# Where the inner products of a two-level Strassen stand, and when the next matrix's quarters are loaded, in a graph layer with gated update

## The chip, the cores and the metric

One core of one Trainium2 chip. The metric is the device time of one execution in microseconds (us); the median of several runs is compared. All arithmetic on the layer's values is in 32-bit floats.

## The reference

A relational graph layer with a gate, on 1250 nodes of 1024 features, 20000 edges of 8 types:

```
h = relu(layernorm(x))
u = h @ root + bias
for r in range(8):
    mask = (edge_type == r)
    sums = segment_sum(h[src] * mask, dst);  cnt = segment_sum(mask, dst)
    u = u + (sums / max(cnt, 1)) @ weight[r]
z = concat(u, h) @ w_gate + b_gate
out = x + tanh(u) * z + h * (1 - z)
```

The kernel multiplies first and gathers after: `y[r] = h @ weight[r]` for all nodes, and each node then adds the rows of y that its edges name, each with its weight.

## The kernel before

**Eleven matrix products.** h (1250 rows, ten blocks of 128) is multiplied by eleven matrices of 1024x1024: the eight of `weight` (s = 0 to 7), `root` (s = 8), the lower half of `w_gate` (s = 9), and at the end the gathered u by its upper half. For each s, `step(s, i)` (line 361) runs over five pairs i = 0 to 4 of two row blocks; a pair is a 2x2 block matrix against the 2x2 quarters of the weight, and `product` (line 262) computes it with seven products (Strassen in Winograd's form) instead of eight. A product is 4 matmuls of 128x512, and each of these, in 32-bit floats, shows as two records in the profile. The seven, by the part of h that they read, and the names that the changed code gives them: A11 first, S1 fifth, S2 sixth, S4 third, S3 seventh, A12 second, A22 fourth. They go into two PSUM banks, b (A11, S2, S3, A22, one on top of the other) and c (S1, S4). ACT copies b after A11 (line 290), S2 (298), S3 (308) and A22 (334), and c after S1 (294); DVE adds c after S4 (303) and the copy of S3 (309). A bank that is added to again must first have been copied. Six banks go round.

**The inner level.** For s > 0 the product A12 of pairs 0 and 1, and that of pairs 2 and 3, are taken together: two row blocks against a quarter of the weight, b21, which `Second` (line 176) splits again into 2x2 and computes with seven inner products of 2 matmuls of 128x256 each (line 210). Its right sums t1 to t4 (128x512, line 194) and left sums s1 to s4 (128x256, line 200) are made by DVE, and its results are added by DVE to the rows of both pairs (line 214). All seven inner products stand in the odd pair (1 or 3), between its outer products; the generator `products` hands them out. The even pair runs A11, S1, S2, S3, S4, A22 with nothing between; the odd pair the same with the inner ones between. Pair 4 and all of s = 0 run all seven outer products in the order A11, S1, S2, S4, S3, A12, A22.

**Weights.** `Factors` (line 123) keeps nine buffers of 1 MB. A matrix needs seven: quarters b11, b12 (in the place of t3), b21, b22 and the sums t1 to t4 (lines 160 to 174, 128x2048 on DVE). The other two are the scratch of `Second`: f0 for its right sums, f1 for its left sums and copies of results. They become b11 and t3 of the next matrix. b11, b22 and b21 are loaded over ACT's queue, b12 over SP's.

**What sets the order.** The program is written out in the order in which each engine runs it. After each outer product (and after two of the inner groups of an odd pair) `done` calls `between(j)`, with j counted from 0 in each pair; `beside` in `step` uses these calls to place everything else:

- call 0 of pair 0: t4 (line 174), then, in pairs 0 and 2, the right sums (pair 0) and the left sums of `Second`
- call 6 of pair 3: both loads b11 and b12 of the next matrix; calls 0 and 3 of pair 4: b22 and b21; calls 3, 4 and 5: t1, t2, t3
- call 6 of an odd pair: the store of the even pair's first row block; the other row blocks are stored when their pair ends
- and at each call the other work's next piece (`on` or `spread`): in s = 0 to 3 the index work (ranks of edges in their nodes: bf16 counts on PE, lines 726 and 777, with work of DVE and ACT around them, lines 708 to 801), and from s = 4 on the gathers of y (POOL's indirect DMA, line 979, and DVE's weighted addition, line 987, through four buffers)

A pair has 7 calls, with s > 0 an even one 6 and an odd one 8 (`calls`, line 355).

Of the kernel before, what the change touches and what calls it, by code (L numbers as in the profile page):

```python
# [19 lines left out]
def tile_rgcn_highway(  # L20
# [31 lines left out]
    nc = tc.nc  # L52
# [9 lines left out]
    Q = D // 2  # L62
    H = Q // 2
    ND = -(-N // P)
    NP = ND // 2
# [3 lines left out]
    R0 = (0, 3, 6, R)  # L69
# [47 lines left out]
    def bank():  # L117
        return psum.tile([P, 512], F32, name="ps", bufs=6)
# [4 lines left out]
    class Factors:  # L123
# [12 lines left out]
        def load_first(self):  # L136
            old = self.old
            if old is None:
                free = wbuf
                self.place = dict(b11=free[0], t3=free[1], b22=free[2], t1=free[3], t2=free[4],  # L140
                                  b21=free[5], t4=free[6])
                self.spare = free[7:]
            else:
                p = old.place
                self.place = dict(b11=old.spare[0], t3=old.spare[1], b22=p["b11"], t1=p["t1"],
                                  t2=p["t2"], b21=p["b22"], t4=p["t3"])
                self.spare = [p["b21"], p["t4"]]
            p = self.place
            self.of = {A11: p["b11"], A12: p["b21"], S4: p["b22"], S1: p["t1"], S2: p["t2"],
                       S3: p["t3"], A22: p["t4"]}  # L150
            self.load(0, 0, p["b11"])
            self.load(0, 1, p["t3"], nc.sync)

        def load_b22(self):
            self.load(1, 1, self.place["b22"])
# [20 lines left out]
    class Second:  # L176
# [14 lines left out]
            self.a11, self.a12, self.a21, self.a22 = [  # L191
                h_op[i + o][:, A12, k:k + 2] for o in (0, 1) for k in (0, 2)]

        def right(self):
            nc.vector.tensor_sub(self.t1, self.b12, self.b11)
            nc.vector.tensor_sub(self.t2, self.b22, self.t1)
            nc.vector.tensor_sub(self.t3, self.b22, self.b12)
            nc.vector.tensor_sub(self.t4, self.b21, self.t2)

        def left(self):  # L200
            nc.vector.tensor_add(self.s1, self.a21, self.a22)
# [4 lines left out]
        def products(self, to):  # L206

            def add(p, a, b, fresh=False):
                for k in range(2):
                    nc.tensor.matmul(p, a[:, k, :], b[:, k, :], start=(fresh and k == 0),  # L210
                                     stop=(k == 1), skip_group_check=True)

            def more(of, a):
                nc.vector.tensor_add(of, of, a)  # L214

            b, c, a = [bank()[:, :H] for _ in range(3)]
            lo, hi = slice(0, H), slice(H, Q)
            add(b, self.a11, self.b11, True)
            nc.scalar.copy(self.p1_p6[:, lo], b)
            add(c, self.s1, self.t1, True)  # L220
            nc.scalar.copy(self.p5, c)
            yield
            add(b, self.s2, self.t2)
            nc.scalar.copy(self.p1_p6[:, hi], b)
            add(c, self.s4, self.b22)
            yield
            add(b, self.s3, self.t3)
            nc.scalar.copy(self.p7, b)
            add(a, self.a12, self.b21, True)
            more(to[0][:, :Q], self.p1_p6)  # L230
            more(to[0][:, hi], c)
            yield
            add(b, self.a22, self.t4)
            more(to[0][:, lo], a)
            more(to[1][:, hi], self.p5)
            more(to[1][:, hi], self.p7)
            yield
            more(to[1][:, lo], b)
            yield

    def transposed(aop, part, of, n):

# [17 lines left out]
            nc.vector.tensor_sub(aop[:, S3], aop[:, A11], aop[:, A21])  # L260

    def product(aop, w, to, between=lambda j: None, last=None, pieces=1, whole=True,
                second=None):

        c11, c12 = to[0][:, :Q], to[0][:, Q:]
        c21, c22 = to[1][:, :Q], to[1][:, Q:]
        step = [0]  # L270

        def add(b, i, fresh=False, at=slice(0, Q)):
            for k in range(KQ):
                nc.tensor.matmul(b[:, at], aop[:, i, k, :], w.of[i][:, k, at],  # L274
                                 start=(fresh and k == 0), stop=(k == KQ - 1),
                                 skip_group_check=True)

        def done():
            between(step[0])
            step[0] += 1  # L280

        def beside(call=False):
            if second is not None:
                next(second)
                if call:
                    done()

        b, c = bank(), bank()
        add(b, A11, True)
        nc.scalar.copy(c11, b)  # L290
        done()
        beside()
        add(c, S1, True)
        nc.scalar.copy(c22, c)  # L294
        done()
        beside(True)
        add(b, S2)
        nc.scalar.copy(c12, b)  # L298
        done()
        beside(True)  # L300
        def p3():
            add(c, S4)
            nc.vector.tensor_add(c12, c12, c)  # L303

        def p7():
# [10 lines left out]
        beside()  # L316
        done()
        if whole:
            d = p7()
        else:  # L320
            p3()
        beside()
        done()
        if whole:
# [17 lines left out]
        done()  # L342

    mats = [weight[r] for r in range(R)] + [root, w_gate[D:, :], w_gate[:D, :]]
    ROOT = R
    NM = len(mats)
    fac = []
# [3 lines left out]
    def paired(s, i):  # L351

        return s > 0 and i < NP // 2 * 2

    def calls(s, i):

        return 7 if not paired(s, i) else 8 if i % 2 else 6

    waiting = {}

    def step(s, i, between=lambda j: None):

        t = [rows.tile([P, D], F32, name="row") for _ in range(2)]
        two = paired(s, i)
        odd = two and i % 2 == 1
        if two and not odd:
            waiting["second"] = Second(fac[s], i)
            waiting["to"] = t[0]

        def put(i, part, t):  # L370
            d = i + part * NP
# [35 lines left out]
        second = waiting["second"].products((waiting["to"], t[0])) if odd else None  # L407
        product(h_op[i], fac[s], t, between=beside, whole=not two, second=second)
        for part in range(2):
            if part or not two or odd:  # L410
                put(i, part, t[part])

    steps = iter([(s, i) for s in range(NM - 1) for i in range(NP)])
# [77 lines left out]
    with ExitStack() as early:  # L491
# [85 lines left out]
        nc.scalar.activation(warm, eps, AF.Sqrt)  # L577
        x0 = [load_x(0, part, pieces=2 - part) for part in range(2)]
        fac[0].load_first()
        fac[0].load_b22()  # L580
        x1 = [load_x(1, 0, scratch(NP - 2, 0))]
        fac[0].load_b21()
# [371 lines left out]
    with ExitStack() as edges_part:  # L954
# [117 lines left out]
        def beside(e, total, s, i, last):  # L1072


            between = spread(e, total, sum(calls(a, b) for a in range(s, last + 1)
                                           for b in range(i if a == s else 0, NP)))
# [113 lines left out]
        def in_turn(*es):  # L1190
            for e in es:
                yield from e
# [62 lines left out]
        def held():  # L1255
# [7 lines left out]
            for add in old + new:  # L1263
                add()

        late = edges(LG, range(HELD, ND), to_last)
        between = spread(in_turn(late, held()), sum(K[LG]) + 2,
                         sum(calls(a, b) for a in range(s, NM - 1)
                             for b in range(i if a == s else 0, NP)))
        while s < NM - 1:  # L1270
            def beside_h(j):
                between(j)
# [69 lines left out]
```

## Time and profile before

| what | value |
|---|---|
| median of 3 runs | 1407.56 us (1400.13 to 1410.84) |
| profiled execution | 1407.21 us, its span 1405.4 us |
| mean granted clock of PE | 0.993 |
| PE busy, matmul records | 1361.3 us, 3786 |
| DVE / ACT / POOL busy | 930.0 / 365.2 / 634.6 us |
| line 274, outer products 128x512 | 2800 records with 16 of 128x256, 1237.9 us |
| line 210, inner products 128x256 | 504 records in two groups, 71.5 + 55.8 us |
| DMA | 272.78 MB, mean 194 GB/s |
| one weight quarter over ACT's queue | 1 MB, median 10.7 us from issue to landing |

The page gives each engine's busy time, the groups of instructions by line with the idle time before them and what ended it, and the DMA issues. A row of the timeline reads: start, length, engine, line, operation, output<-inputs, shape, count, and in brackets the idle time before it with the instruction that ended it. PE's matmuls overlap and their ends are modelled; from start to start is the safer measure. The matrices start about 120 us apart: s = 1 near 150, s = 4 near 537, s = 8 near 1020.

### The profile page before, as it was taken

How to read it: one execution, taken by the hardware profiler on the slowest of the kernel's cores; microseconds unless marked ns; L12 is line 12 of the kernel's file. 1: busy time of each engine (PE TensorE's matmuls, PEld its weight loads, DVE VectorE, ACT ScalarE, POOL GpSimd, SP SyncE). 2: the span in 40 equal slices, each digit the busy share in tenths (PEclk: the TensorE clock that was granted, in tenths of full speed). 3: DMA queues.
4: the chain of work that ended last, by engine and by line, in shares of the span. 5: the costliest groups of instructions: out<-in, count | busy, mean ns of one | idle time of the engine just before them, and what ended most of it. 6: DMA issues, size and time to landing. Idle time of an engine off the chain costs nothing.

```text
span 1405.4 us, 12717 instructions
## 1 busy us (share of the span) xinstructions
PE 1361.3 (97%) x3786; PEld 659.0 (47%) x3786; DVE 930.0 (66%) x1842; ACT 365.2 (26%) x793; POOL 634.6 (45%) x567
## 2 busy tenths in 40 slices
PE   7999799999999999999999999999989999999997
PEld 3444354445544444454444445454434545454443
DVE  6946776897768817555555775655367475657985
ACT  3335465656631111111111111111111111121220
POOL 0003555566561543655674364544327333424641
PEclk9999999999999999999999999999999999999999
DMA  8764344846463375369679547777849753676761
GB/s 299 278 199 112 96 106 119 226 94 142 83 193 102 62 206 138 84 207 270 194 245 326 203 167 243 290 260 270 301 123 344 246 189 111 211 249 215 271 234 57
DMA packets 110011, 272.78 MB, mean 194 GB/s; under 512 B 25906, under 2 KB 27936, under 8 KB 109808
## 3 DMA queue, kind: packets, MB, share of 16 engines
q0 software_dynamic: 48864, 128.60, 28.6%
q1 hardware_dynamic: 45232, 111.86, 26.3%
q10 hardware_dynamic: 15840, 31.46, 7.3%
q8 instruction: 30, 0.49, 0.1%
q14 instruction: 45, 0.37, 0.1%
HBM read 214.20 MB, written 80.65 MB: 210 GB/s over the span
## 4 chain that ended last, share of the span: by engine, by line
PE 45%; issue 21%; DMA 10%; DVE 10%; POOL 8%; ACT 1%; POOLq 0%; DVEq 0%; ACTq 0%
PE ps L274 39%; DMA got<-y,idx 7%; PE ps L210 5%; POOL got L979 4%; DMA u<-u_dram,node 2%; DVE u L987 2%; POOL got L436 1%; POOL u_dram L442 1%; DMA got<-hr_dram,node 1%; DVE w L170 0%; DMA node_dram<-ids,pos_i 0%; PE ps_n L726 0%; DVE row L303 0%; DVE w L166 0%; DVE row L214 0%
## 5 line engine op out<-in xcount | busy, mean ns | idle before, releaser
L274 PE MATMUL ps<-w,h_op 128*128 128x512 f32 x2800 | 1237.9, 597 | 19.1 <-ACT row L298 15.2
L274 PEld LDWEIGHTS ps<-w,h_op 128*128 128x128 f32 x2800 | 527.4, 191 | 633.9 <-issue 593.3
L987 DVE SCALAR_TENSOR_TENSOR u<-got,w_of,u 128x1024 f32<-128x1024 f32 (+1 forms) x192 | 245.9, 1282 | 200.2 <-DMA got<-y,idx 198.0
L979 POOL DMA_INDIRECT got<-y,idx x202 | 253.5, 1255 | 242.7 <-DVE u L987 146.0
L805 POOL DMA_INDIRECT table<-row_col,at_i x157 | 176.0, 1121 | 163.2 <-DVE at_i L801 83.3
L334 ACT COPY row<-ps 128x512 f32<-128x512 f32 x50 | 29.3, 585 | 264.9 <-PE ps L274 259.2
L309 DVE TENSOR_TENSOR row<-row,part 128x512 f32<-128x512 f32 x55 | 37.9, 690 | 78.9 <-ACT part L308 78.6
L308 ACT COPY part<-ps 128x512 f32<-128x512 f32 x55 | 32.2, 585 | 196.5 <-PE ps L274 196.3
L303 DVE TENSOR_TENSOR row<-row,ps 128x512 f32<-128x512 f32 x55 | 37.6, 684 | 66.9 <-PE ps L274 46.5
L290 ACT COPY row<-ps 128x512 f32<-128x512 f32 x55 | 32.1, 585 | 165.6 <-PE ps L274 153.6
L210 PE MATMUL ps<-w,w 128*128 128x256 f32 x288 | 71.5, 381 | 0.0
L294 ACT COPY row<-ps 128x512 f32<-128x512 f32 x55 | 32.2, 585 | 146.9 <-PE ps L274 137.0
L298 ACT COPY row<-ps 128x512 f32<-128x512 f32 x55 | 32.2, 585 | 146.5 <-PE ps L274 146.5
L442 POOL DMA_INDIRECT u_dram<-u,node x20 | 29.6, 1480 | 77.9 <-DVE u L987 65.4
L210 PEld LDWEIGHTS ps<-w,w 128*128 128x128 f32 x288 | 54.1, 190 | 19.0 <-issue 13.4
L791 DVE SCALAR_TENSOR_TENSOR junk<-k_bc,key_col,before 128x128 f32<-128x128 int32 x157 | 54.9, 350 | 4.2
L210 PE MATMUL ps<-w,h_op 128*128 128x256 f32 x216 | 55.8, 381 | 1.2 <-DVE row L303 1.2
L731 DVE TENSOR_TENSOR seen<-seen,ps_n 128x110 f32<-128x110 f32 x157 | 42.2, 269 | 19.7 <-PE ps_n L726 15.4
L473 POOL DMA_INDIRECT node_dram<-ids,pos_i x30 | 37.8, 1261 | 38.4 <-issue 36.8
L708 ACT ACTIVATE is_lo<-io,less_lo 128x128 bf16<-128x128 f32 x157 | 50.1, 391 | 0.9 <-DVE row L309 0.9
L210 PEld LDWEIGHTS ps<-w,h_op 128*128 128x128 f32 x216 | 40.6, 190 | 20.6 <-issue 14.3
L859 DVE SCALAR_TENSOR_TENSOR junk<-v_bc,val,one 128x1280 bf16<-128x1280 f32 x30 | 46.5, 1550 | 2.4 <-DMA v_bc<-val_dram 1.7
(180 smaller groups left out, 946.7 us busy)
## 6 DMA issues: line engine op xcount, KB each, us to landing
y<-row SPq DMA_DIRECT2D x72, 512.0 KB, 7.6
w<-in_L_gnn_weight_dram ACTq DMA_DIRECT2D x21, 1024.0 KB, 10.7
w<-in_L_gnn_weight_dram SPq DMA_DIRECT2D x11, 1024.0 KB
k_bc<-keys_dram SPq DMA_DIRECT2D x39, 256.0 KB, 4.4
l_bc<-los_dram SPq DMA_DIRECT2D x39, 256.0 KB, 5.7
w<-in_L_gnn_w_gate_dram ACTq DMA_DIRECT2D x6, 1024.0 KB
h_dram<-h_op SPq DMA_DIRECT2D x9, 512.0 KB, 6.6
hr_dram<-row SPq DMA_DIRECT2D x9, 512.0 KB, 4.5
```

The source lines that it names most:

```text
L210: nc.tensor.matmul(p, a[:, k, :], b[:, k, :], start=(fresh and k == 0), stop=(k == 1), skip_group_check=True)
L274: nc.tensor.matmul(b[:, at], aop[:, i, k, :], w.of[i][:, k, at], start=(fresh and k == 0), stop=(k == KQ - 1), skip_group_check=True)
L309: nc.vector.tensor_add(c22, c22, d)
L442: ins = nc.gpsimd.indirect_dma_start(out=of, out_offset=bass.IndirectOffsetOnAxis(ap=at, axis=0), in_=frm, in_offset=None)
L473: ins = nc.gpsimd.indirect_dma_start(out=node_dram[g][:, :], out_offset=bass.IndirectOffsetOnAxis(ap=pos_i[:, g, d:d + 1], axis=0), in_=id ...
L708: nc.scalar.activation(is_lo[:, i, :], io, AF.Abs, bias=less_lo[:, c0 + i:c0 + i + 1])
L731: nc.vector.tensor_add(seen[j][:, i, :], was, p[:, i, :])
L791: nc.vector.scalar_tensor_tensor(junk, o["k_bc"][:, i, :], key_col[:, c:c + 1], before, op0=OP.is_equal, op1=OP.mult, accum_out=rank[:, c: ...
L805: ins = nc.gpsimd.indirect_dma_start(out=table[:, :], out_offset=bass.IndirectOffsetOnAxis(ap=at_i[:n, i:i + 1], axis=0), in_=row_col[:n, ...
L859: nc.vector.scalar_tensor_tensor(junk, v_bc[:, g, :], val[:, c:c + 1], one.to_broadcast([P, KEYS]), op0=OP.is_gt, op1=OP.mult, accum_out=p ...
L979: nc.gpsimd.indirect_dma_start(out=t[:n], out_offset=None, in_=y[g][:, :], in_offset=bass.IndirectOffsetOnAxis(ap=at[:n, d, k:k + 1], axis=0),
L987: nc.vector.scalar_tensor_tensor(u[:n], t[:n], w, u[:n], op0=OP.mult, op1=OP.add)
```

## The change

- In pair 0 the inner `second` (a12 by b21) moves from pair 1 to stand between S2 and S3. Pair 1 has the others at new places: first and fifth after A11, sixth and third after S1, seventh after S2, fourth after S3.
- Pairs 2 and 3 are divided: in pair 2, first and fifth stand between S2 and S3, sixth and third after S3, seventh after S4, fourth after A22; in pair 3, `second` stands between S2 and S3, and DVE's additions of the others to pair 3's rows come after A11.
- Each pair has 7 calls now; pair 0's extra one is after the inner second's place, pair 1's after sixth and third, pair 2's at its end, pair 3's after the inner second.
- The left sums for pair 2 move from call 0 of pair 2 to call 6 of pair 1. In s = 1 to 3 the right sums stand one at each of calls 0 to 3 of pair 0 and the left sums at call 4; from s = 4 on all stay at call 0.
- b11 of the next matrix is loaded at call 0 of pair 3 and b12 at call 2 (both at call 6 before); t1, t2, t3 are made at calls 1, 3, 4 of pair 4 (3, 4, 5 before). b22 and b21 stay at calls 0 and 3.
- The store of an even pair's first row block stands after S4 in pair 1 as before, and after S3 in pair 3.

```diff
-            self.load(0, 1, p["t3"], nc.sync)
+
+        def load_next(self):
+            self.load(0, 1, self.place["t3"], nc.sync)
...
-        def right(self):
-            nc.vector.tensor_sub(self.t1, self.b12, self.b11)
-            nc.vector.tensor_sub(self.t2, self.b22, self.t1)
-            nc.vector.tensor_sub(self.t3, self.b22, self.b12)
-            nc.vector.tensor_sub(self.t4, self.b21, self.t2)
+        def right(self, k):
+            to, a, b = ((self.t1, self.b12, self.b11), (self.t2, self.b22, self.t1),
+                        (self.t3, self.b22, self.b12), (self.t4, self.b21, self.t2))[k]
+            nc.vector.tensor_sub(to, a, b)
...
+        def sixth(self):
+            self.add(self.b, self.s2, self.t2)
+            nc.scalar.copy(self.p1_p6[:, H:], self.b)
+            self.add(self.c, self.s4, self.b22)
+
+        def seventh(self):
+            self.add(self.b, self.s3, self.t3)
+            nc.scalar.copy(self.p7, self.b)
+
+        def fourth(self):
+            self.add(self.b, self.a22, self.t4)
+
+        def second(self):
+            self.a = bank()[:, :H]
+            self.add(self.a, self.a12, self.b21, True)
...
+        def filled(name):
+            if fill and name in fill and fill[name]():
+                done()
...
         add(b, S2)
         nc.scalar.copy(c12, b)
         done()
-        beside(True)
...
+        filled("sixth")
         if whole:
             p3()
-        else:
-            p7()
...
+        else:
+            d = p7()
+            p3()
...
         def beside(j):
...
-            if two and not odd and j == 0:
-                if i == 0:
-                    waiting["second"].right()
-                waiting["second"].left()
-            if odd and j == 6:
-                put(i - 1, 0, waiting["to"])
-            if (s, i, j) == (0, 0, 3) or (s > 0 and i == NP - 2 and j == 6):
+            if two and i == 0:
+                sums(j)
+            if two and (i, j) == (1, 6):
+                Second(fac[s], 2).left()
+            if (s, i, j) == (0, 0, 3) or (s > 0 and (i, j) == (3, 0)):
                 new.load_first()
+            if (s, i, j) == (0, 0, 3) or (s > 0 and (i, j) == (3, 2)):
+                new.load_next()
             if i == NP - 1:
                 if j == 0:
                     new.load_b22()
+                elif j == 1:
+                    new.make_t1()
                 elif j == 3:
                     new.load_b21()
-                    new.make_t1()
+                    new.make_t2()
                 elif j == 4:
-                    new.make_t2()
-                elif j == 5:
                     new.make_t3()
             between(j)
...
+        def sums(j):
+            e = waiting[0][0]
+            for k in range(4) if s > R0[1] and j == 0 else (j,) if s <= R0[1] and j < 4 else ():
+                e.right(k)
+            if j == (0 if s > R0[1] else 4):
+                e.left()
+
+        fill = {}
+        if two:
+            e, to = waiting[i - i % 2]
+            if i == 0:
+                fill = dict(sixth=lambda: (e.second(), e.second_to_first(to)))
+            elif i == 1:
+                fill = dict(first=lambda: e.first(),
+                            fifth=lambda: (e.sixth(), True),
+                            sixth=lambda: (e.seventh(), e.to_first(to), 0)[-1],
+                            seventh=lambda: (e.fourth(), e.to_second(t[0]), 0)[-1],
+                            third=lambda: (e.fourth_to_second(t[0]), put(i - 1, 0, to), 0)[-1])
+            elif i == 2:
+                fill = dict(sixth=lambda: e.first(),
+                            seventh=lambda: e.sixth(),
+                            third=lambda: (e.seventh(), e.to_first(to), 0)[-1],
+                            fourth=lambda: (e.fourth(), True))
+            else:
+                fill = dict(first=lambda: (e.to_second(t[0]), e.fourth_to_second(t[0]), 0)[-1],
+                            sixth=lambda: (e.second(), True),
+                            seventh=lambda: (e.second_to_first(to), put(i - 1, 0, to), 0)[-1])
```

`to_first`, `to_second`, `second_to_first` and `fourth_to_second` are DVE's additions of the inner results to the rows, the same five instructions for each two pairs as before.

More of the change, by code (lines that the diff above doesn't have):

```diff
@@ L204, in left @@
             nc.vector.tensor_sub(self.s4, self.a12, self.s2)
[L206 to L239, printed above, removed]
@@ new lines, in add, with first @@
+        def add(self, p, a, b, fresh=False):
+            for k in range(2):
+                nc.tensor.matmul(p, a[:, k, :], b[:, k, :], start=(fresh and k == 0),
+                                 stop=(k == 1), skip_group_check=True)
+        def first(self):
+            self.b, self.c = [bank()[:, :H] for _ in range(2)]
+            self.add(self.b, self.a11, self.b11, True)
+            nc.scalar.copy(self.p1_p6[:, :H], self.b)
+            self.add(self.c, self.s1, self.t1, True)
+            nc.scalar.copy(self.p5, self.c)
@@ new lines, in sixth, with to_first @@
+        def sixth(self):
[10 more added lines that the diff above has]
+            self.add(self.a, self.a12, self.b21, True)
+        def to_first(self, to):
+            nc.vector.tensor_add(to[:, :Q], to[:, :Q], self.p1_p6)
+            nc.vector.tensor_add(to[:, H:Q], to[:, H:Q], self.c)
@@ L241, in transposed, with second_to_first, to_second, fourth_to_second @@
+        def second_to_first(self, to):
+            nc.vector.tensor_add(to[:, :H], to[:, :H], self.a)
+        def to_second(self, to):
+            nc.vector.tensor_add(to[:, H:Q], to[:, H:Q], self.p5)
+            nc.vector.tensor_add(to[:, H:Q], to[:, H:Q], self.p7)
+        def fourth_to_second(self, to):
+            nc.vector.tensor_add(to[:, :H], to[:, :H], self.b)
     def transposed(aop, part, of, n):
@@ L262, in product @@
     def product(aop, w, to, between=lambda j: None, last=None, pieces=1, whole=True,
-                second=None):
+                fill=None):
         c11, c12 = to[0][:, :Q], to[0][:, Q:]
@@ L280, in done @@
             step[0] += 1
[L282 to L295, printed above, removed]
-        beside(True)
[L297 to L300, printed above, removed]
+        def filled(name):
+            if fill and name in fill and fill[name]():
+                done()
         def p3():
@@ L303, in p3 @@
             nc.vector.tensor_add(c12, c12, c)
+            done()
+            filled("third")
         def p7():
@@ L309, in p7 @@
             nc.vector.tensor_add(c22, c22, d)
-            return d
+            done()
+            filled("seventh")
+            return d
+        b, c = bank(), bank()
+        add(b, A11, True)
+        nc.scalar.copy(c11, b)
+        done()
+        filled("first")
+        add(c, S1, True)
+        nc.scalar.copy(c22, c)
+        done()
+        filled("fifth")
+        add(b, S2)
+        nc.scalar.copy(c12, b)
+        done()
+        filled("sixth")
         if whole:
             p3()
-        else:
-            p7()
-        beside()
-        done()
-        if whole:
-            d = p7()
[L320 to L324, printed above, removed]
+            d = p7()
             a = bank()
@@ L342, in product @@
         done()
+        filled("fourth")
     mats = [weight[r] for r in range(R)] + [root, w_gate[D:, :], w_gate[:D, :]]
@@ L353, in paired @@
         return s > 0 and i < NP // 2 * 2
-    def calls(s, i):
-        return 7 if not paired(s, i) else 8 if i % 2 else 6
     waiting = {}
@@ L364, in step @@
         two = paired(s, i)
[L365 to L368, printed above, removed]
+        if two and i % 2 == 0:
+            waiting[i] = Second(fac[s], i), t[0]
         def put(i, part, t):
@@ L397, in beside @@
                     new.load_b22()
+                elif j == 1:
+                    new.make_t1()
                 elif j == 3:
                     new.load_b21()
-                    new.make_t1()
+                    new.make_t2()
                 elif j == 4:
-                    new.make_t2()
-                elif j == 5:
                     new.make_t3()
             between(j)
-        second = waiting["second"].products((waiting["to"], t[0])) if odd else None
-        product(h_op[i], fac[s], t, between=beside, whole=not two, second=second)
+        def sums(j):
[24 more added lines that the diff above has]
+                            seventh=lambda: (e.second_to_first(to), put(i - 1, 0, to), 0)[-1])
+        product(h_op[i], fac[s], t, between=beside, whole=not two, fill=fill)
         for part in range(2):
-            if part or not two or odd:
+            if part or not two or i % 2:
                 put(i, part, t[part])
@@ L579, in tile_rgcn_highway @@
         fac[0].load_first()
+        fac[0].load_next()
         fac[0].load_b22()
@@ L1072, in beside @@
         def beside(e, total, s, i, last):
-            between = spread(e, total, sum(calls(a, b) for a in range(s, last + 1)
-                                           for b in range(i if a == s else 0, NP)))
+            between = spread(e, total, 7 * ((last - s) * NP + NP - i))
             while s <= last:
@@ L1266, in tile_rgcn_highway @@
         late = edges(LG, range(HELD, ND), to_last)
-        between = spread(in_turn(late, held()), sum(K[LG]) + 2,
-                         sum(calls(a, b) for a in range(s, NM - 1)
-                             for b in range(i if a == s else 0, NP)))
+        between = spread(in_turn(late, held()), sum(K[LG]) + 2, 7 * ((NM - 2 - s) * NP + NP - i))
         while s < NM - 1:
```

## The prediction

> **What bounds the kernel now.** I read the page first (busy time of each engine), then the waits of PE, then PE's timeline around each wait, and last DVE's timeline, since DVE is what PE waits for.
>
> ```profile
> PE 1361.3 (97%) x3786; PEld 659.0 (47%) x3786; DVE 930.0 (66%) x1842; ACT 365.2 (26%) x793; POOL 634.6 (45%) x567
> PE ps L274 <- ACT row L298: 15.2, 17, 4.2
> PE ps L274 <- DVE w L162: 3.6, 1, 3.6
> PE ps_q L777 <- DVE own L782: 2.9, 1, 2.9
> PE ps_n L726 <- DVE seen L731: 2.8, 1, 2.8
> PE ps L210 <- DVE row L303: 1.2, 1, 1.2
> ```
>
> PE is the bound, and the change neither adds nor removes a matmul. All it can win is PE's idle time and the slow matmuls after it. The chain of waits names gathers in the second half, but DVE there mostly waits for PE or for its own gathers without PE stopping. So I count PE's own gaps.
>
> ```profile
> 424.58 1.88 PE L274 MATMUL ps<-w,h_op 128*128 128x512 f32 x4
> 427.14 14.00 PE L274 MATMUL ps<-w,h_op 128*128 128x512 f32 x32 [0.68 <-ACT row L298]
> 440.98 1.03 PE L210 MATMUL ps<-w,h_op 128*128 128x256 f32 x4
> 441.84 1.03 PE L210 MATMUL ps<-w,w 128*128 128x256 f32 x4
> 457.32 17.33 PE L274 MATMUL ps<-w,h_op 128*128 128x512 f32 x40
> 475.32 14.00 PE L274 MATMUL ps<-w,h_op 128*128 128x512 f32 x32 [0.68 <-ACT row L298]
> ```
>
> Ends are modelled, so starts are what count. The 40 matmuls from 457.32 take (17.33 - 0.59)/39 = 0.429 us each from start to start; a 512-wide product (8 records) takes 3.44. The next could start at 457.32 + 40 x 0.429 = 474.48 and starts at 475.32: 0.84 us lost, of which the row shows 0.68 as idle. This is an even pair: S3 follows S2 into the same bank and must wait for ACT's copy (L298, 0.59). Four 256-wide records (one inner product) take 441.84 - 440.98 = 0.86.
>
> **Even pairs.** The 0.68 occurs 14 times, in pairs 0 and 2 of matrices 3 to 9 (the rest of the 15.2 lies in matrices 1 and 2, below). In the changed order an inner product (0.86 in pair 0, 1.72 in pair 2) stands between S2 and S3: 0.84 is covered. Gain 14 x 0.84 = 11.8. The cover is thin in pairs 0, 1 and 3 (0.86 against 0.84; the odd pairs had 1.72 before), so 27 places from matrix 1 on may keep something: nothing, or at most 0.1 each, 2.7. I take 0.5 back, near nothing, since nothing else stands on ACT there outside the index work.
>
> **The matrix boundary.** At the start of matrix 8 PE waits for t1:
>
> ```profile
> 1021.83 2.60 DVE L987 SCALAR_TENSOR_TENSOR u<-got,w_of,u 128x1024 f32<-128x1024 f32 x2 [16.93 <-DMA got<-y,idx]
> 1024.36 0.68 DVE L303 TENSOR_TENSOR row<-row,ps 128x512 f32<-128x512 f32 x1
> 1024.95 2.28 DVE L162 TENSOR_TENSOR w<-w,w 128x2048 f32<-128x2048 f32 x1
> 1027.29 10.21 PE L274 MATMUL ps<-w,h_op 128*128 128x512 f32 x16 [3.65 <-DVE w L162]
> ```
>
> The weights are not late: t1 is queued on DVE at call 3 of pair 4, behind two gather additions that wait 16.93 us. PE loses 3.8 us, and the next 16 records take 10.21 where 16 x 0.429 + 0.17 = 7.0 would do: 3.1 more. The granted clock of 1027 to 1034 is 0.54. In the new order t1 is queued at call 1, ahead of both additions, so its wait is gone. Next late is t2, behind them at call 3: about 1024.4 + 0.68 + 2.28 = 1027.4, against S1's end at 1023.5 + 3.44 = 1026.9: 0.5 lost. Gain 3.8 + 3.1 - 0.5 = 6.4. The Trainium skill ("TensorE: Matmul & The Clock Gate", HAM oscillation) puts an idle window over about 3.4 us at half clock for another such window: 1.7 us of loss. The row shows 3.1, and I use the row. By the rule the gain would be 5.0.
>
> The loads' earlier issue by itself I cost at nothing. The Trainium skill ("Trainium Kernel Development and Optimization", Key Constraints) speaks against it: all queues share 16 DMA engines, so a load moved to pair 3 takes from the gathers there what it frees in pair 4. The same 4 MB are moved either way. On ACT the b11 load waits for the inner fourth, which PE has passed; on SP the b12 load waits for DVE's additions in pair 3, and behind it stands one store of y, which needs later DVE work anyway. b22 must now land by call 3 instead of 4: 10.3 us after its issue, where ACT's weight loads took 10.7 (median) to 13.7. So DVE may stand 0 to 4 us at t2; S2 needs t2 only 17 us later, and that slack hides it. The inner second needs b21 20 us after its issue: hidden.
>
> The 1.2 of L210 <- L303 (1.4 by starts) is a bank that pair 1 needs before pair 0's addition has freed it. In the new order the reusing product stands two or more products later: gain 1.4.
>
> **The index stage (matrices 1 and 2).** PE waits on bursts of DVE work:
>
> ```profile
> 153.65 2.28 DVE L174 TENSOR_TENSOR w<-w,w 128x2048 f32<-128x2048 f32 x1
> 159.85 1.17 DVE L731 TENSOR_TENSOR seen<-seen,ps_n 128x110 f32<-128x110 f32 x4
> 161.07 0.36 PE L726 MATMUL ps_n<-is_at,is_lo 128*128 128x110 bf16 x4 [2.75 <-DVE seen L731]
> 165.02 0.57 ACT L298 COPY row<-ps 128x512 f32<-128x512 f32 x1
> 165.64 1.22 PE L274 MATMUL ps<-w,h_op 128*128 128x512 f32 x1 [4.20 <-ACT row L298]
> ```
>
> Between 153.65 and 159.85 DVE makes t4, four right sums and four left sums (6.2 us) ahead of the counts. Loss by starts: 2.9 + 4.4, and 2.2 of slow matmuls: 9.5. Matrix 2 loses 3.0 + 1.6 at 295, and single waits 1.2 (218) and 0.7 (350). Now one right sum stands at each call and left at call 4: the burst is t4 + 0.69 = 3.0, so L731 runs near 156.6 and L754 ends near 158.2. But ACT's 4.0 us of bookkeeping (is_lo, to_lo) waits for that and stands ahead of L298, so the copy ends near 162.9 against a slot for S3 at 159.2 (S2, the inner second, the place): 3.7 lost and about 1.3 of slow clock. Gain there 4.5, plus 4.6 + 1.2 + 0.7 for the others: 11.0. Against it: bookkeeping calls that stand only 0.86 apart now (three pairs in each matrix) and the left sums at the end of pair 1. The trace shows calls 1.72 apart with little loss; I bound the cost between 0 and 5 and take 2, nearer to the 1.72 rows. Net 9.0.
>
> **What it adds.** Pair 2's left sums (4 x 0.42) must be ready at its first fill: queued after pair 1's last product, needed 3 x 3.44 + 0.43 = 10.8 later; before it was over 20. DVE runs late behind gathers. From the start of the copy of pair 2's first product to L201, matrices 1 to 9 show -0.6, -1.6, 5.4, -2.9, 14.4, 4.7, 0.3, 3.4, -1.3. Only matrix 5 is beyond:
>
> ```profile
> 718.62 0.75 DVE L985 TENSOR_SCALAR u<-got,w_of 128x1024 f32<-128x1024 f32 x1 [1.81 <-DMA got<-y,idx]
> 723.41 1.28 DVE L987 SCALAR_TENSOR_TENSOR u<-got,w_of,u 128x1024 f32<-128x1024 f32 x1 [4.04 <-DMA got<-y,idx]
> 724.61 0.42 DVE L201 TENSOR_TENSOR w<-h_op 128x256 f32<-128x256 f32 x1
> ```
>
> Now it stands ahead of the last addition, so near 719.4: s1 at 719.8 against 710.2 + 6.88 + 0.43 = 717.5. Wait 2.3, with slow clock up to 5.5; 0 if DVE is less late by then. I take 2.
>
> **Sum.** -11.8 + 0.5 - 6.4 - 1.4 - 9.0 + 2.0 = -26.1. The profiled execution took 1407.2 (span 1405.4), the median of the runs is 1407.56: the same within 0.4. 1407.2 - 26.1 = 1381.1, said as **1381.0**.
>
> **The rivals.**
> 1. As summed, 1381 (own range 1374 to 1389): chance 0.66.
> 2. Only the even pairs gain. ACT's order keeps the index waits (gain 2 instead of 9), and at matrix 8 t2 takes t1's place with slow clock (gain 2 instead of 6.4): 1381 + 7 + 4.4 = 1392.4. For: in the index stage ACT, not DVE, is last before S3. Against: the waits at 295 have no ACT in them. 0.12.
> 3. The cover is short and the left sums wait: 2.7 - 0.5, and 2.3 in each of matrices 3 to 9 instead of 2 in all (+14.1): 1381 + 16.3 = 1397. For: matrix 5. Against: six of seven late times are under 6. 0.07.
> 4. Slower. The same left sums wait 3 us or more in all nine matrices and each wait brings 3.1 of slow clock: 9 x 6.1 - 2 = 53: 1434. It decides from 26.1/9 = 2.9 lost in each matrix, that is from a lateness of L201 of about 7 everywhere plus the clock; one of nine shows that. 0.03.
> 5. More: the index waits all go (16.5) and nothing is added: 1381 - 7.5 - 2 - 0.5 = 1371. For: all four are bursts that are now cut. Against: ACT's 4.0 us ahead of L298. 0.12.
>
> **Numbers.** A measurement of this kernel tells about 1% from no change: below 1393.5 is faster, above 1421.6 slower. Faster: cases 1 and 5 and half of case 2, 0.84; within: the other half and case 3, 0.13; slower 0.03. The range 1370 to 1396 leaves out cases 3 and 4 and a tail of 5.
>
> **What would show it.** In the new profile: L298's counterpart gone from PE's waits or under 2 us in all; no wait for t1 at matrix 8, clock there 1.0; the right sums one by one in matrices 1 to 3 and PE's idle time from 150 to 440 cut by more than half; a PE wait on the left sums at pair 2 of matrix 5 at most. Wrong would be: repeated PE waits on left sums or on the copy after S2, or a DVE standing at t2 for b22 so long that S2 waits.

## The result and the profile after

The changed kernel takes 1397.41 us (median of 20 runs, 1392.21 to 1404.80), the kernel before 1406.80 (20 runs, 1400.13 to 1413.52): ratio 0.9936, 95% interval 0.9919 to 0.9952. That is 9.4 us, within 1%, where 1381.0 us in all, a gain of 26.1, was predicted. The profiled execution took 1399.42, its span 1397.6, 7.8 less than before. Clock: 0.990 (0.993 before).

First the busy time of the page and the waits of PE, after the change. Line 282 is the outer matmul (274 before), 209 the inner one, 319 the copy after S2 (298 before), 315 the copy after S1, 240 DVE's addition of the inner second to its row.

```profile
PE 1358.3 (97%) x3786; PEld 658.3 (47%) x3786; DVE 928.8 (66%) x1842; ACT 365.2 (26%) x793; POOL 630.6 (45%) x567
PE ps L282 <- DVE row L240: 10.2, 2, 7.8
PE ps L282 <- ACT row L315: 9.2, 1, 9.2
PE ps_q L804 <- ACT to_lo L795: 2.2, 3, 1.4
PE ps_n L753 <- DVE seen L758: 2.1, 2, 1.0
PE ps L282 <- ACT row L319: 0.2, 1, 0.2
```

The copy after S2 fell from 15.2 us to 0.2 and the wait for t1 is gone. But two waits stand on top that were not there: 10.2 and 9.2. I counted PE's losses in the two profiled executions from start to start again, slow matmuls behind a wait included:

| place | before | after |
|---|---|---|
| even pairs, matrices 3 to 9 | 11.8 | 0 |
| index stage (matrices 1 to 3) | 16.5 | 5.4 |
| boundary of matrix 8, t1 | 7.0 | 0 |
| bank in matrix 5 | 1.4 | 0 |
| start and end of the kernel | 5.9 | 3.4 |
| new: pair 1 of matrix 5, at 667 us (line 240) | | 2.6 + 1.8 |
| new: pair 4 of matrix 7, at 988 (line 315) | | 9.4 + 2.1 |
| new: pair 1 of matrix 8, at 1040 (line 240) | | 7.9 + 2.5 |
| other | 0.6 | 0.3 |
| sum | 43.2 | 35.4 |

The second number of a new wait is the slow clock after it. The sums differ by 7.8, as the spans do, so nothing is missing: 34 us were won and 26 came back. (Of the 34, 2.5 stand at the start and end, which the change does not touch and which vary by 2 to 3 us between executions.)

The gathers come in three groups of matrices. The first is gathered beside matrices 4 and 5, the second beside 6 and 7; each leaves its sums in DRAM as u, block by block of 128 nodes. The third is gathered from matrix 8 on. All that came back stands in this part of the kernel: from the first outer product of matrix 4 to the first of matrix 9, 611.0 us before and 620.6 after. The changed kernel is slower there.

The stretch before 998 us in time order, all engines:

```profile
966.94 1.03 PE L209 MATMUL ps<-w,h_op 128*128 128x256 f32 x4
967.80 20.84 PE L282 MATMUL ps<-w,h_op 128*128 128x512 f32 x48
...
972.30 1.82 POOL L468 DMA_INDIRECT u_dram<-u,node  x1 [3.80 <-DVE u L1014]
980.68 0.95 POOL L462 DMA_INDIRECT u<-u_dram,node  x1 [6.56 <-DMA u_dram<-u,node]
981.94 1.00 POOL L1006 DMA_INDIRECT got<-y,idx  x1 [0.30 <-issue]
...
989.20 1.28 DVE L1014 SCALAR_TENSOR_TENSOR u<-got,w_of,u 128x1024 f32<-128x1024 f32 x1 [14.67 <-DMA got<-y,idx]
...
992.20 0.41 DVE L240 TENSOR_TENSOR row<-row,ps 128x256 f32<-128x256 f32 x1
...
997.25 0.59 ACT L315 COPY row<-ps 128x512 f32<-128x512 f32 x1 [14.81 <-DMA y<-row]
...
997.89 2.93 PE L282 MATMUL ps<-w,h_op 128*128 128x512 f32 x3 [9.25 <-ACT row L315]
```

Read it from the bottom. PE waits for ACT's copy 315. That copy fills a row buffer and waits for the store of what the buffer held: the first block of pair 2, which needs DVE's addition 240. The addition ran at 992.20; the inner product that it adds (line 209) had been made at 967, but it is queued behind gather additions (line 1014), the first of which stood 14.67 us for its gathered row. And that row was late because POOL, in order, had these three instructions (468, 462, 1006): write the finished block's sum u to DRAM, read the next block's u from DRAM (waits 6.56 for the write), and only then the next gather. At 1040 the last link is another one:

```profile
1023.97 1.03 PE L209 MATMUL ps<-w,h_op 128*128 128x256 f32 x4
...
1026.49 2.29 DVE L176 TENSOR_TENSOR w<-w,w 128x2048 f32<-128x2048 f32 x1 [2.57 <-DVEq L1146]
...
1039.51 1.03 PE L209 MATMUL ps<-w,w 128*128 128x256 f32 x4
...
1041.06 1.28 DVE L1014 SCALAR_TENSOR_TENSOR u<-got,w_of,u 128x1024 f32<-128x1024 f32 x1 [8.28 <-issue]
...
1043.39 1.28 DVE L1014 SCALAR_TENSOR_TENSOR u<-got,w_of,u 128x1024 f32<-128x1024 f32 x1 [1.05 <-DMA got<-y,idx]
...
1046.63 1.28 DVE L1014 SCALAR_TENSOR_TENSOR u<-got,w_of,u 128x1024 f32<-128x1024 f32 x1 [1.96 <-DMA got<-y,idx]
...
1047.83 0.41 DVE L240 TENSOR_TENSOR row<-row,ps 128x256 f32<-128x256 f32 x1
...
1048.30 4.64 PE L282 MATMUL ps<-w,h_op 128*128 128x512 f32 x5 [7.76 <-DVE row L240]
```

Pair 1's S1 takes the bank of pair 0's inner second (made at 1023.97), and the addition that frees it stands behind three gather additions. These belong to the third group, and the stand of 8.28 us ahead of them is not what the change brought: with u stored late (below) it is 8.52, and PE does not wait. But there t4 (line 176) ran 7.9 us ahead of the inner second (1001.35 and 1009.22), and here 2.5 behind it. The difference, 10.4, is the wait and its slow clock: DVE comes late out of the second group.

### The profile page after: what moved, and what is told of

Its sections match the earlier page's. It is cut to its first block, busy times and chain, and to the rows that moved or that the text cites. A ratio compares the mean times of both kernels' runs of the same rounds, so it can differ in the third digit from the quotient of the medians.

```text
span 1397.6 us, 12703 instructions
## 1 busy us (share of the span) xinstructions
PE 1358.3 (97%) x3786; PEld 658.3 (47%) x3786; DVE 928.8 (66%) x1842; ACT 365.2 (26%) x793; POOL 630.6 (45%) x567
## 4 chain that ended last, share of the span: by engine, by line
PE 54%; issue 14%; DMA 12%; DVE 9%; POOL 5%; ACT 1%; POOLq 0%; DVEq 0%; ACTq 0%
PE ps L282 48%; DMA got<-y,idx 8%; PE ps L209 6%; DMA u<-u_dram,node 2%; DVE u L1014 2%; POOL got L1006 1%; POOL got L462 1%; DMA w<-in_L_gnn_weight_dram 1%; POOL u_dram L468 1%; DVE junk L818 0%; DVE w L172 0%; DMA got<-hr_dram,node 0%; DMA h_op<-z_dram,node 0%; DVE seen L758 0%; PE ps_n L753 0%
## 5 line engine op out<-in xcount | busy, mean ns | idle before, releaser
L282 PE MATMUL ps<-w,h_op 128*128 128x512 f32 x2800 | 1236.8, 596 | 19.8 <-DVE row L240 10.2
L1006 POOL DMA_INDIRECT got<-y,idx x202 | 250.2, 1238 | 255.6 <-DVE u L1014 159.4
```

Of the source, the lines that this page charges most:

```text
L1006: nc.gpsimd.indirect_dma_start(out=t[:n], out_offset=None, in_=y[g][:, :], in_offset=bass.IndirectOffsetOnAxis(ap=at[:n, d, k:k + 1], axis=0),
```

## The experiments

Theories, as the expectations name them. **T**: two new buffer dependencies, the bank and the row buffer; give each another buffer and the time appears. **R**: gathers and DVE set the pace of matrices 4 to 8, and PE waits somewhere whatever is freed. **L**: the weight loads moved to pair 3 slow the gathers. Later R was split: **G**, DVE stands at gathers that have not landed; **V**, DVE simply has too much work. Ratios are to the kernel before on the same chip, where it took 1410.72 us (the two buffers and the loads), 1413.27 (no gathers, both edits of u's turnover, one place ahead) or 1407.58 (the rest), so times of different runs compare by their ratios; the expectations in us were made for 1407. "Matrices 4 to 8" is the stretch named above, of the profiled execution. Where a line was added ahead of them, profile lines of an experiment are one higher (283 for 282).

**A bank of its own.** The inner second takes a PSUM bank that is idle from matrix 4 on:

```
-            self.a = bank()[:, :H]
+            self.a = (psum.tile([P, 512], F32, name="ps_q", bufs=1) if self.own else bank())[:, :H]
```

> Edit: the changed kernel, but from matrix 4 on the inner second product takes the PSUM bank of the index work's place step, which is idle by then, and no longer one of the six that go round. Theory T (the gain on PE was had, and given back in two new places where PE waits for DVE additions that are queued behind gather additions: the bank of pair 0's inner second, and the row buffer of pair 2's first block): PE's waits on L240's row go (10.2 us and about 4 us of slow clock in the profile of the changed kernel), the wait behind ACT's copy of S1 stays; 1397 - 10 to 14 = 1383 to 1387. Rival R (the gathers are the bound from matrix 4 to 8, PE only waits somewhere else instead): 1394 to 1398. Rival L (the weight loads moved to pair 3 slow the gathers): 1394 to 1398, since the loads stay where they are.

Measured: 1399.70, ratio 0.9914 (0.9881 to 0.9947). PE's waits:

```profile
PE ps L283 <- ACT row L316: 9.4, 1, 9.4
...
PE ps L210 <- DVE w L203: 4.0, 1, 4.0
```

Line 240 is gone from the list, as planned, and pair 2's left sums of matrix 5 (line 203), for which PE had not waited, now hold it. Matrices 4 to 8 take 612.3 us, 8.3 less than in the changed kernel, where line 240 cost 14.8.

**A row buffer more.** Pair 2's first block gets a fifth buffer in matrices 4 to 7 (the bias tile, whose load moves to the root matrix):

```
+        t = [more_row[0] if more_row and s < ROOT and i == 2 and part == 0
+             else rows.tile([P, D], F32, name="row") for part in range(2)]
```

> Edit: the changed kernel with a fifth row buffer for the first row block of pair 2 in matrices 4 to 7 (the tile that holds the bias later; the bias is loaded at matrix 8). Theory T: ACT's copy of S1 in pair 4 no longer waits for the store of that block, so the 9.2 us wait at matrix 7 and its 2.3 us of slow clock go, where they occur; the bank waits stay; 1397 - 5 to 11 = 1386 to 1392. Rival R: 1394 to 1398. Rival L: 1394 to 1398.

Measured: 1408.17, ratio 0.9986 (0.9965 to 1.0006). The wait of 9.2 is gone; line 240 grew from 10.2 to 16.4, of which 12.4 stand in matrix 8, at whose start PE also waits 4.3 for t2 (line 168). Matrices 4 to 8 take 623.0. So what the buffer frees is lost one matrix later. Why the median of 22 runs lies another 5 us above the profiled execution (1403.41) stays open.

**Both.**

> Edit: the bank of e1 and the row buffer of e2 together. Theory T: both new waits go and the forecast's time is nearly reached: 1372 to 1380. Rival R: PE waits for the next thing that DVE frees, and the time is within 5 us of the changed kernel: 1392 to 1398. Rival L: as R.

Measured: 1403.46, ratio 0.9942 (0.9920 to 0.9965). Neither wait is there; the left sums (7.9 in two waits) and the copy after S2 (5.7 in matrix 8) are. Matrices 4 to 8 take 614.5. T falls: each dependency was real, but of the 26 us that came back, the two buffers bring 6 in that stretch. (The medians show little of it: in the profiled executions of the first and the third of these runs matrix 1, which they leave as it is, took 6 to 7 us longer than in the changed kernel's.) The rest is taken by the next thing that DVE hands to PE.

**Loads and t1 to t3 back in their old places.**

```
-            if (s, i, j) == (0, 0, 3) or (s > 0 and (i, j) == (3, 0)):
+            if (s, i, j) == (0, 0, 3) or (s > 0 and (i, j) == (3, 6)):
...
-                elif j == 1:
-                    new.make_t1()
                 elif j == 3:
                     new.load_b21()
-                    new.make_t2()
+                    new.make_t1()
```

> Edit: the changed kernel with the loads of the next matrix's b11 and b12 back at call 6 of pair 3 and t1, t2, t3 back at calls 3, 4, 5 of pair 4; the inner products stay at their new places. Theory T: the two new waits do not come from the loads and stay; t1 is late again at matrix 8 where DVE stands: 1395 to 1405. Rival L: the gathers of pair 3 are no longer slowed, the new waits shrink by more than half: 1383 to 1391.

Measured: 1422.87, ratio 1.0065 (1.0032 to 1.0097), so 18 us slower than the changed kernel (1.0065 - 0.9936 of 1407) and slower than T and L had it. DVE's waits for gathers did not shrink (181.8 from 600 to 1100 us, 166.7 with the loads early). L falls; the early loads and sums together are worth more than the 6.4 that I gave them.

**No gathers.** Now the cover itself. The additions stay; what they wait for goes:

```
-            t = got()
-            nc.gpsimd.indirect_dma_start(
-                out=t[:n], out_offset=None, in_=y[g][:, :],
...
+            t = bias_bc
```

> The changed kernel with all gathers of rows of y left out (also those of the last group, and the late load of b_gate): each of the 155 additions keeps its place, shape and 1.28 us on DVE, but reads a tile that lies in SBUF, so that it waits for no transfer. u is still written to and read from DRAM. The output is therefore not the reference's. Theory G (DVE stands still at gather additions whose rows have not landed, and what PE needs next is queued behind them): the three new waits of matrices 5, 7 and 8 (4.3, 11.5 and 10.4 us with the slow clock behind them) go, nothing takes their place, and the time is 1370 to 1377. Theory V (DVE has too much work in these matrices, gathers or not): waits of the same sum stand elsewhere, 1390 to 1398.

Measured: 1380.99, ratio 0.9781 (0.9756 to 0.9807), the profiled execution 1376.12. In us that is above the range of G; by its ratio, on 1407, it is 1376 and inside. The additions as the page lists them:

```profile
L1010 DVE SCALAR_TENSOR_TENSOR u<-bias_bc,w_of,u 128x1024 f32<-128x1024 f32 (+1 forms) x192 | 245.4, 1281 | 12.2 <-DMA u<-u_dram,node 5.3
```

There are 192 of this form (not 155), with the same 245 us of DVE work, and between 300 and 1200 us the list of PE's waits is empty. Matrices 4 to 8 take 594.0. V falls, G stands.

> The same edit on the kernel before: all gathers of rows of y left out, the additions kept, reading a tile in SBUF. Theory G: the waits that gathers don't cause stay, that is the even pairs' 11.8 us, the bank's 1.4 and the index stage's 16.5; the boundary at matrix 8 (7.0) goes, so 1396 to 1402, and the changed kernel without gathers is 23 to 28 us faster than this one, as the prediction's sum had it. Theory V: this kernel loses nothing more either, but the two differ by 10 us as they do with gathers.

Measured: 1399.84, ratio 0.9912 (0.9885 to 0.9940). The even pairs' waits are there (13 of 14). The pair differs by 18.9 by medians (24.3 by the profiled spans, of which 4 are a loss in matrix 3 that this one execution alone has), less than the 23 to 28 that I expected, and it should be: without gathers the kernel before has no boundary wait and no bank wait either, so of the prediction's sum 6.4 + 1.4 can't show in this difference: 26.1 - 7.8 = 18.3. Matrices 4 to 8 take 602.2 here and 594.0 in the changed kernel without gathers: 8 us of PE's gaps in this part, which the change did remove.

**The turnover of u.** The round trip write, read, gather can be taken out of POOL's way with the whole computation kept. A DRAM tensor of its own for the second group's sums, and a block's sum written behind four gathers of the next block instead of two:

```
-            of = u_dram if g else None
+            of = (None, u_dram, u2_dram)[g]
...
-                    if k == min(1, last):
-                        leave()
-                        if d != blocks[-1]:
-                            ahead = new_u(d + 1, of, g)
+                    if k == min(1, last) and d != blocks[-1]:
+                        ahead = new_u(d + 1, of, g)
+                    if k == min(3, last):
+                        leave()
```

> The changed kernel, complete, with the turnover of u taken out of the gather chain: the second group writes its sums to a DRAM tensor of its own (so a read of u waits for no write of the same group), and a block's sum is written behind four gathers of the next block, not two. Theory G: POOL's 38 us of waits for the write and part of its 70 us for the last addition go, gathers land earlier, the row-buffer wait of 9.4 us at matrix 7 goes with its slow clock, and no equal wait takes its place: 1384 to 1390. If the gathers' own latency, and not the turnover, is what holds DVE, 1394 to 1400. Theory V: 1394 to 1400.

Measured: 1385.78, ratio 0.9805 (0.9781 to 0.9830). By its ratio that is 1380 on 1407, a little better than G had it. No PE wait is left from 300 to 1200 us, and matrices 4 to 8 take 594.0, as without gathers, though every transfer is there. So neither DVE's work nor the amount that the DMA moves held the kernel. Then each half alone:

> One half of the run that stores u late: only the DRAM tensor of its own for the second group's sums; a sum is still written behind two gathers. POOL's waits for the write ahead of a read (38 us) go, its waits at the write for the last addition (70 us) stay. If the round trip through DRAM is what makes DVE stand at gathers: nearly the whole gain of the run with both, ratio 0.981 to 0.985 to the kernel before. If the gathers queued behind POOL's waiting write are: 0.990 to 0.994, as the changed kernel.

Measured: 1388.25, ratio 0.9855 (0.9825 to 0.9884): between the two answers, at the edge of the first: a little over half of the way from the changed kernel (0.9936) to the run below (0.9783). POOL's waits for the write are gone but for one of 3.2, those at the write stay (78.3 in all). PE still waits 5.6 for line 240 (here 241) and 2.2 for left sums; matrices 4 to 8 take 604.3.

> The other half: u_dram is written and read by the same group as in the changed kernel, but a block's sum is written behind four gathers of the next block. A read of u then stands ahead of the write that it used to wait for, and waits only for one that is a block older. If POOL's place at the write (with the gathers queued behind it) decides: both kinds of POOL's waits fall, 0.980 to 0.985. If only the tensor of its own helps: 0.990 to 0.994.

Measured: 1377.72, ratio 0.9783 (0.9754 to 0.9813), the lowest ratio of all (the interval overlaps that of the run with both edits), 30 us below the kernel before and 20 below the changed one, by one `if` moved. Matrices 4 to 8 take 594.0 again. Lines of POOL's waits from 600 to 1100 us, of the changed kernel and then of this one:

```profile
POOL got L1006 <- DVE u L1014: 78.9, 39, 10.4
POOL u_dram L468 <- DVE u L1014: 69.7, 18, 11.4
POOL u L462 <- DMA u_dram<-u,node: 38.1, 9, 8.1
```

```profile
POOL got L1006 <- DVE u L1014: 147.5, 59, 10.4
...
POOL u_dram L468 <- DVE u L1014: 20.3, 2, 10.4
POOL u_dram L468 <- DMA u<-u_dram,node: 8.9, 4, 3.6
...
POOL u L462 <- DMA u_dram<-u,node: 6.2, 3, 3.2
```

The waits at the write and for the write (108 us) shrink to 35, of which 8.9 are new: the write now waits for a read. POOL waits as long as ever, but now for a free gather buffer, that is with all four buffers taken by gathers issued ahead. DVE's side, same window, of the changed kernel and of this one:

```profile
DVE u L1014 <- DMA got<-y,idx: 166.7, 55, 14.7
```

```profile
DVE u L1014 <- DMA got<-y,idx: 67.4, 38, 7.2
```

**The inner piece one place ahead.** Would a smaller repair of the order on DVE have done?

```
             nc.vector.tensor_add(c12, c12, c)
-            done()
             filled("third")
+            done()
```

(and the same behind the seventh)

> The changed kernel with the inner piece that stands behind the third and behind the seventh product issued ahead of that product's own step call, not behind it, so that the additions of the inner product (the one that frees the bank of its second product, and the one that the store of the row buffer waits for) stand ahead of one more gather addition on DVE and on SP. Theory T (order of the queue by one place is what makes the new waits): the waits of 2.6 and 7.9 us for the bank and 9.4 for the row buffer shrink by one gather addition each, 2 to 7 us: about 1385. Theory G: an addition that is moved ahead by one place still waits for gathers that were issued earlier, the sum of waits stays within 5 us: 1392 to 1400.

Measured: 1405.29, ratio 0.9945 (0.9922 to 0.9969). The waits on line 240 are 11.0, on 315 5.0, and the left sums wait 3.5: the sum is 19.5 against 19.4. As G has it, also by its ratio (1399 on 1407).

**Late store in the kernel before.**

> Both edits of the turnover of u made in the kernel before. Its own PE waits at gather-bound additions are small (boundary of matrix 8, 7.0 us with the slow clock, and the bank's 1.4): theory G gives 1396 to 1401, ratio 0.992 to 0.997, so that the change is worth 20 to 24 us where the gathers run ahead, against 9 where they don't. If the gathers' turnover costs the kernel before as much as the changed one (25 us), 0.98 to 0.985, and the change is worth the same 9 with it.

Measured: 1395.15, ratio 0.9915 (0.9885 to 0.9946). It wins 12, just more than the range had. In the profile 8.8 of them stand in matrices 4 to 8 (611.0 to 602.2: the boundary and the bank) and most of the rest at the start, which the edits don't touch. With both edits in both kernels the change is worth 15.5 (0.9915 - 0.9805 of 1407), with the late store alone in the changed one 18.6 (0.9783); as the kernels were, 9. The expectation had 20 to 24 or 9, so it lies between.

**Late store, loads back.**

> The changed kernel with u's turnover as in the run that stores u late, and with the loads of the next matrix's first quarters and the sums t1 to t3 put back to their places in the kernel before. The prediction priced this part at 6.4 us, all at matrix 8's boundary. If the gathers were what made it cost 25 us in the run that put the loads back: 4 to 9 us slower than the run that stores u late, ratio 0.984 to 0.988. If the loads' place pays by itself all along: 0.992 or above.

Measured: 1387.73, ratio 0.9850 (0.9821 to 0.9879), 6 us slower than the run with the same store and the loads early (0.9850 - 0.9805), with intervals that just overlap. With the gathers running ahead the early loads and sums are worth about as much as the prediction's 6.4; without, 18. But the agreement with 6.4 is chance: in the profile PE waits for line 240 (here 241, 5.5 us) and for left sums (1.7), matrix 2 takes 3.2 us longer, and t1 and t2, on which the 6.4 was counted, keep nobody waiting.

## Why the prediction was wrong

**The step that failed** is the one on which all the others stood: "The chain of waits names gathers in the second half, but DVE there mostly waits for PE or for its own gathers without PE stopping. So I count PE's own gaps." PE's gaps say what bounds the kernel at its present pace. They do not say how far the next engine is behind. The trace of before had one half of that number, the time from the first write of u to the last (the gather chain of two groups); the other half took a run without gathers. The starts of these writes in four runs (before, after, and the same two without gathers):

```profile
L442 POOL DMA_INDIRECT u_dram<-u,node x20: 983/1032/3357, 602.8 to 1036.7; - x20
L468 POOL DMA_INDIRECT u_dram<-u,node x20: 987/1035/3358, 588.6 to 1024.2; - x20
L442 POOL DMA_INDIRECT u_dram<-u,node x20: 962/1126/3322, 606.3 to 1024.1; - x20
L468 POOL DMA_INDIRECT u_dram<-u,node x20: 962/1044/3322, 591.8 to 1000.8; - x20
```

| us | first to last write of u: before | after | matrices 4 to 8: before | after |
|---|---|---|---|---|
| as they are | 433.9 | 435.6 | 611.0 | 620.6 |
| gathers left out | 417.8 | 409.0 | 602.2 | 594.0 |
| both edits of u's turnover | 415.9 | 408.1 | 602.2 | 594.0 |
| u stored late alone | | 408.3 | | 594.0 |
| a tensor of its own alone | | 419.7 | | 604.3 |
| a bank of its own | | 434.0 | | 612.3 |
| a row buffer more | | 434.6 | | 623.0 |
| bank and row buffer | | 430.5 | | 614.5 |
| one place ahead | | 434.5 | | 621.0 |
| loads and sums back | | 451.6 | | 636.5 |

At PE's pace the stretch would take 418 before and 409 after. The gather chain took 434 to 436 in both, and 430 to 435 in four variants of the changed kernel that leave the gathers as they are. So before the change the chain was already 16 us late at its end, of which PE paid 8.4 (boundary and bank); the rest was not yet charged to anybody. The change took 9 us from PE's side and nothing from the chain's: it is 27 us late, and PE pays 26. Shown: waits move when one is removed (the bank, the row buffer, both), go when the gathers go, and go when u is stored late with all gathers kept. The new places of the products have a share in it, since they tie PE to additions that it did not wait for before: with the bank freed PE pays 18 and not 26. That 434 is a fixed length of the chain is not shown; the run with the loads back has 451.6.

Term by term:

- **Even pairs**, -11.8 + 0.5: 11.8 came, and the thin cover held: 0.2 is left in one place, in the index stage. Right.
- **Matrix boundary**, -6.4: line 164 (t1) made nobody wait at matrix 8, nor did t2. (The row's slow clock is 3.2, 10.21 - 7.03, where the prediction has 3.1.) But 7.9 + 2.5 stands in pair 1 of matrix 8, behind late gathers again. The local reading was right, and worthless as long as the gathers' lateness stayed.
- **Bank**, -1.4, "the reusing product stands two or more products later": wrong in mechanism. In pair 1 S1 gets the bank of pair 0's inner second, as PE's wait for line 240 shows. Time to spare was counted in products of PE; it had to be counted in DVE's queue, where two (matrix 5) and three (matrix 8) gather additions stood ahead. The 1.4 of matrix 5 came, but the term was to stay at that: 14.8 stand against it (2.6 + 1.8 + 7.9 + 2.5).
- **The row buffer**, put at nothing without a reason, since it is not in the sum at all: 9.4 + 2.1. The store of pair 2's first block needs DVE's last addition, and pair 4's S1 needs the buffer.
- **Index stage**, -9.0: -11.1 in the profiled execution, where 5.4 is left at 157, 273 and 287 us and nothing of the 2 us for bookkeeping calls 0.86 apart can be seen. But this execution was the luckiest: matrix 1 took 129.8 us in it and 131.2 to 137.1 in seven runs whose edits leave that matrix as it is, against 138.3 to 138.8 in the three of the kernel before; matrix 2 took 128.3 to 128.4 against 131.1 to 131.4. So 4 to 11 us came, and 9.0 lies within. (The four losses of 9.5, 4.6, 1.2 and 0.7 make 16.0, not the 16.5 that rival 5 takes.)
- **Left sums**, +2.0: none in the profiled execution, 4.0 in the run with a bank of its own.
- **Slow clock.** The prediction took 3.1 us a wait from its row. Waits of 2.6, 9.4 and 7.9 brought 1.8, 2.1 and 2.5 (granted clock 0.68, 0.68 and 0.60 over the 5.3 to 6 us behind them): less than my row, and not in order of the wait's length. The 1.7 that I set beside it is an estimate of mine, half of another stretch of about 3.4 us, and a little low here. The example of the Trainium skill ("TensorE: Matmul & The Clock Gate", HAM oscillation) has 1.67 us at half clock after each longer gap and counts half of it as lost, which is less than any of these waits cost.

Rival 3 had a time near the result (1397) by another mechanism: 2.7 us of thin cover and left sums in every matrix. Neither is in the trace, so its agreement is chance. The queue behind late gathers was in no rival, although the fence on t1 showed it: 16.93 us of DVE standing at one addition.

The Trainium skill ("DMA: Bandwidth & Descriptors", Anatomy of one DMA — SWDGE) says that a DMA's wait for a semaphore happens on the issuing sequencer, ahead of dispatch. In the trace the read of u waited 6.56 us on POOL at 974, and four gathers that then went out one after the other, 981.94 to 985.84, stood behind it. Read with that in mind, POOL's waits on the write of u in the kernel before, from 600 to 1100 us, were the place to look:

```profile
POOL u_dram L442 <- DVE u L987: 65.4, 17, 10.2
...
POOL u L436 <- DMA u_dram<-u,node: 36.5, 9, 8.4
```

**What stays open:** the split of the turnover. The run with a tensor of its own removes the 38 us for the read and gains a little over half; the late store, which also removes most of the other 70, gains all. The run with both lies between them in ratio (0.9805), with an interval that overlaps both of theirs. By matrices 4 to 8 the late store and both edits are equal. And the median of the run with a fifth row buffer stays unexplained.

## What to carry to other kernels

Before you add up the gaps of the bounding engine, measure what the next engine's chain would take in the same stretch: by its own row of waits, or by a run with its inputs left out. If that chain is as long as the stretch, removing gaps moves the wait and not the end. A queue that carries both a producer's round trip and the prefetches behind it is worth reordering first: on top of the change, one store moved behind two more gathers gave more here than the change itself.

## What the runs showed of the hardware

**A round trip on a queue.** POOL's write of a block of u to DRAM (128 rows of 4 KB) and the read that waits for it took 8.4 us from issue to issue at 972.30, and 3.6 to 9.9 in the eight such places of the second group. In the last blocks of a group, of three to five gathers each, the additions that could cover it take at most 6.4 us (five of 1.28).

**A slow clock after short waits.** After the wait of 2.6 us at 667 the granted clock was 0.68 from 670.2 to 675.5, and 1.8 us were lost. After one of 3.0 at 681 in the run with the loads back it was 1.00, and 0.1 was lost. Over the profiled executions of all runs, from 420 us on: of the six waits of 2.1 to 3.0 us, two (2.1 and 2.6) cost 1.8 us more and four 0.1; eight shorter ones, from 1.4, cost 0.1 (one 0.8), and eighteen from 3.6 to 12.6 cost 1.8 to 3.2, in no order by length.
